# The last pair's feed-forward by batch, and the small steps of the norms moved between VectorE and GpSimd

## The chip, the cores and the metric

The kernel runs on one core of a Trainium2 chip. The metric is device time in microseconds (us) of one execution. The core's engines work in parallel, each through its own instructions in order: TensorE (PE; its weight loads are listed apart as PEld), VectorE (DVE), ScalarE (ACT), GpSimd (POOL), and SyncE (SP), which here only issues DMAs. Engines wait for one another through semaphores. Matrix products land in PSUM, which has eight banks of 128 partitions by 512 fp32 values; everything else lies in SBUF.

## The reference

The input is 16 batches of 256 tokens with 128 features. Twelve layers of linear attention (16 heads of 8, no softmax) are followed by a norm, a gated feed-forward network with hidden size 384, and a second norm:

```python
for i in range(12):
    q, k, v = split(x @ Wqkv[i].T + bqkv[i])        # 16 heads of 8
    att = einsum('bhqd,bhkd->bhqk', q, k) / sqrt(8)
    x = (att @ v) @ Wproj[i].T + bproj[i] + x
x = layernorm(x0 + x)                                # first norm
h = silu(x @ Wg.T / 127) * (x @ Wu.T / 127)
x = layernorm(x + h @ Wd.T / 127)                    # second norm
# layernorm(x) = (x - mean) / sqrt(var + 1e-5), over the 128 features
```

## The kernel before

The 16 batches are handled as eight pairs, numbered p = 0 to 7. A pair is 512 tokens: K = 4 chunks of 128 tokens. Since attention without softmax is linear, the twelve layers work on one small 128x128 map for each batch (a matrix `tst`, with one column for the offset); the tokens come in again only at the end, in `ffn(p)` (L567). The change concerns that function alone.

`ffn(p)` goes through these steps, all 512 tokens of a pair at once:

1. The map is transposed and copied, its offset column is split into three bf16 parts, and PE multiplies the tokens by it (L658). The result `pr` has tokens on the partitions and is already centred, because the last layer's weights had their mean taken off.
2. First norm, `norm(pr, True)` (L579): the statistics are two `bn_stats` on DVE, each over two chunks (L595). POOL then adds eps to the variance (`ve`, L602) and raises it to the power -0.5 (`rs`, L603). The scaling by `rs` is one DVE instruction (L608) or four ACT instructions (L613).
3. PE transposes the result back to features on the partitions (L664). To keep fp32 precision in fast products, every value that PE streams is split in two: a rounded high part (`xh`, a copy) and the rest (`xl`, a subtraction, L667).
4. For each of the three blocks of 128 hidden features: four products of 512 columns (gate and up, high and low part, L674 and L675), Silu on ACT (L677), the multiplication by up on DVE (L678), the split of the product into `hh` (a copy on ACT or DVE, L201 or L203) and `hl` (a subtraction on POOL or DVE, L206), and two products into the down sum (L686 and L687). The first block also adds `xl` times 127 (L685).
5. DVE scales the down sum and adds `xh` (L689). PE transposes back to tokens on the partitions (L695).
6. Second norm, `norm(po, False, po2)`: statistics, eps and power as in step 2. DVE then forms `nb`, the negated mean times the power (L621), and ACT scales each chunk with it, four instructions (L617), after which SP stores 256 KB (L701). For the last pair the transposed result lies in two banks: DVE scales chunks 0 and 1 (L615) and ACT chunks 2 and 3 (L617), and SP and ACT store 128 KB each.

Many of these values lie in buffers that earlier stages used, so the profile shows other names: `kv` is the normed value, `yhl` is `xh`, `thl` is `xl`, `xt` and `qgv` are the gated values.

The order of the work is not the order in which this code is written. Each step is registered with a planner (`Plan`, L92) with a booked duration for every engine that may do it, what it reads and writes, and a due time `prio`. `Plan.run` (L116) is a list scheduler: it takes the step that can start first, and among those that can start then the one with the smallest rank, puts it on the engine that it books to finish it first, and emits it there. The rank (L142) is the due time less a ten-thousandth of the booked nanoseconds that still follow the step on its longest path, with 300 ns for each step of the path:

```python
(_, end, e), o = min(((b, o) for b, o in found if b[0] <= first),
    key=lambda x: (x[1].prio - TAILW * x[1].tail, -x[1].tail, x[1].n))
```

A layer is one unit of due time; pair p of the feed-forward has 11 + 0.15 p. The eight PSUM banks are handed out by the planner too. All engines then run the emitted order as it is, so an instruction that waits holds back whatever was emitted behind it on its engine.

Of the kernel before, what the change touches and what calls it, by code (L numbers as in the profile page):

```python
# [9 lines left out]
F32 = mybir.dt.float32  # L10
# [42 lines left out]
TAILW = 0.0001  # L53

# [134 lines left out]
def linear_attention_ffn_kernel(ctx: ExitStack, tc: tile.TileContext, x, xt, wall, wq0, bias, wg, wu, wd, out):  # L189
# [360 lines left out]
    for p in range(NP):  # L550
# [4 lines left out]
            "ve": new(f"ve{p}", [4]), "rs": new(f"rs{p}", [4]), "nb": new(f"nb{p}", [4]), "st": new(f"st{p}", [K, 3]),  # L555
# [11 lines left out]
    def ffn(p, prio):  # L567
# [5 lines left out]
        v = {n: Val() for n in ("cr", "cp", "cq", "tt", "st", "rs", "nb", "x1", "xh", "xl", "sg0", "sg1", "hh0", "hh1", "hl0", "hl1")}  # L573
# [5 lines left out]
        def norm(src, centred, other=None):  # L579


            xs, rows = t("x1"), lambda: bank(src)
            cut = lambda a, k: a[:, k * C : (k + 1) * C]
            row = lambda k: cut(bank(other if other and k >= K // 2 else src), k)

            def stats(e):
                if e == ACT:
                    for k in range(K):
                        nc.scalar.activation(cut(xs, k), row(k), AF.Square, accum_out=t("st")[:, k, 2:3])
                else:  # L590

                    for k in range(0, K, 2):
                        b = bank(other if other and k else src)
                        both = b[:, k * C : (k + 2) * C].rearrange("p (k c) -> p c k", c=C)
                        nc.vector.bn_stats(t("st")[:, k : k + 2, :].rearrange("p k s -> p (k s)"), both)  # L595
            costs = {DVE: K // 2 * (dve(2 * C) + 70)}
            if centred:
                costs[ACT] = K * 485
            op(costs, stats, [src, *([other] if other else [])], [v["st"], v["x1"]])

            def rstd(e):
                nc.gpsimd.tensor_scalar(t("ve"), t("st")[:, :, 2], 1.0 / C, EPS, ALU.mult, ALU.add)  # L602
                nc.gpsimd.tensor_tensor(t("rs"), t("ve"), mhalf, ALU.pow)  # L603
            op({POOL: 1220}, rstd, [v["st"]], [v["rs"]])

            def scale(e, ks=range(K)):
                if centred and e == DVE:
                    nc.vector.tensor_tensor(chunks(xs), chunks(rows()), t("rs").unsqueeze(2).to_broadcast([128, K, C]), ALU.mult)  # L608
                    return
                for k in ks:  # L610
                    d, r, rs = cut(xs, k), row(k), t("rs")[:, k : k + 1]
                    if centred:
                        nc.scalar.activation(d, r, AF.Copy, scale=rs)  # L613
                    elif e == DVE:
                        nc.vector.tensor_scalar(d, r, t("st")[:, k, 1:2], rs, ALU.subtract, ALU.mult)  # L615
                    else:
                        nc.scalar.activation(d, r, AF.Identity, bias=t("nb")[:, k : k + 1], scale=rs)  # L617
            if centred:
                costs = {DVE: dve(N), ACT: K * act(C, False, 1)}
            else:  # L620
                op({DVE: 75}, lambda e: nc.vector.scalar_tensor_tensor(t("nb"), t("st")[:, :, 1], -1.0, t("rs"), ALU.mult, ALU.mult), [v["rs"], v["st"]], [v["nb"]])  # L621
                costs = {ACT: K * act(C, False, 2)}
            if not other:
                op(costs, scale, [src, v["rs"], v["st"], v["nb"]], [v["x1"]])
                return [v["x1"]]

            ends = [Val(), Val()]
            op({DVE: 2 * 319}, lambda e: scale(e, range(2)), [src, v["rs"], v["st"], v["nb"], v["x1"]], [ends[0]])
# [128 lines left out]
```

## Time and profile before

| | |
|---|---|
| median of 3 runs | 311.49 us (311.48 to 311.62) |
| profiled execution, its own time | 312.4 us |
| its span, first to last instruction | 310.7 us |
| mean granted TensorE clock | 0.988 |
| PE busy | 297.8 us, 96% |
| PEld busy | 272.5 us, 88% |
| DVE busy | 234.5 us, 75% |
| ACT busy | 212.5 us, 68% |
| POOL busy | 134.0 us, 43% |
| chain that ended last | PE 89%, DVE 5%, POOL 2%, issue 1%, DMA 1% |

The span is the time between the first and the last instruction; the execution's own time has what lies around it too. A row of the timeline gives start and length in us, engine, source line, operation, what it writes and reads (partitions x elements), how often, and in brackets how long the engine stood idle before it and what ended that. Instructions of one engine overlap in the records, since the next is started before the last has left the pipeline: how far two starts lie apart is then what an instruction costs its engine, and its length is what a reader of its result waits for. The chain of waits is followed back from the last instruction, at each step to what released it.

### The profile page before, as it was taken

To read this page: it belongs to the slowest core of one execution; us is meant where nothing else is said; L and a number is where in the kernel's file an instruction comes from. 1 tells how busy PE (TensorE), PEld (TensorE's weight loads), DVE (VectorE), ACT (ScalarE), POOL (GpSimd) and SP (SyncE) were. 2 spreads that over 40 slices of the span, in tenths; PEclk is the share of its full clock that TensorE was granted. 3 is DMA by queue.
4 is the path that set the end of the run, shared out by engine and by line. 5 is a ranking of instruction groups with operands and counts; after the bars stand their busy time and mean duration, and the time that the engine had idled before them with its cause. 6 is when DMAs were issued, how large, how long until landed. Compare 5 with 4: busy or idle time off the path is not lost.

```text
span 310.7 us, 12884 instructions
## 1 busy us (share of the span) xinstructions
PE 297.8 (96%) x5374; PEld 272.5 (88%) x5374; DVE 234.5 (75%) x706; ACT 212.5 (68%) x541; POOL 134.0 (43%) x218
## 2 busy tenths in 40 slices
PE   7997999999999999999999999999999999999971
PEld 7997999999999999989999999999999998887840
DVE  0788786977687676866768777676768798999982
ACT  2567797677677677666776767876876566657683
POOL 5337350545423454234531445312330459737781
PEclk9999999999999999999999999999999999999995
DMA  7464630211202012030120201300000000001124
GB/s 226 110 189 120 188 80 28 63 28 41 50 2 75 18 36 53 2 90 2 37 53 4 70 20 27 82 27 4 2 2 3 5 0 2 0 0 36 35 72 131
DMA packets 22490, 15.66 MB, mean 50 GB/s; under 512 B 1952, under 2 KB 19872, under 8 KB 22432
## 3 DMA queue, kind: packets, MB, share of 16 engines
q1 hardware_dynamic: 21872, 14.62, 17.1%
q8 instruction: 42, 0.69, 1.0%
q10 hardware_dynamic: 560, 0.22, 0.3%
q14 instruction: 16, 0.13, 0.2%
HBM read 8.02 MB, written 2.10 MB: 33 GB/s over the span
## 4 chain that ended last, share of the span: by engine, by line
PE 89%; DVE 5%; POOL 2%; issue 1%; DMA 1%; ACT 0%; POOLq 0%; DVEq 0%; ACTq 0%
PE bank L452 14%; PE bank L431 8%; PE bank L511 8%; PE bank L433 7%; PE bank L432 7%; PE bank L439 5%; PE bank L496 5%; PE bank L528 4%; PE bank L529 4%; PE bank L530 4%; PE bank L440 3%; PE bank L441 3%; PE bank L674 3%; PE bank L675 3%; PE bank L333 2%; PE bank L658 2%
## 5 line engine op out<-in xcount | busy, mean ns | idle before, releaser
L206 POOL TENSOR_TENSOR thl<-tst,thl 128x260 fp32r<-128x260 f32 x88 | 64.4, 763 | 122.9 <-ACT thl L201 122.9
L201 ACT COPY qgv<-bank 128x256 f32<-128x256 f32 x167 | 59.6, 376 | 20.8 <-PE bank L441 13.9
L201 ACT COPY kv<-bank 128x512 f32<-128x512 f32 (+1 forms) x89 | 51.0, 573 | 23.1 <-PE bank L433 16.4
L431 PE MATMUL bank<-whl,thl 128*128 128x256 f32 x176 | 51.8, 294 | 0.0
L433 PE MATMUL bank<-whl,thl 128*128 128x256 f32 x176 | 49.5, 281 | 0.0
L432 PE MATMUL bank<-whl,thl 128*128 128x256 f32 x176 | 49.4, 281 | 0.0
L452 PE MATMUL bank<-kv,g 128*128 128x128 f32 x352 | 46.4, 275 | 0.0
L535 DVE TENSOR_TENSOR tst<-bank,tst 128x260 f32<-128x260 f32 x96 | 36.7, 424 | 10.2 <-PE bank L530 8.6
L452 PEld LDWEIGHTS bank<-kv,g 128*128 128x128 f32 x352 | 42.9, 191 | 0.4 <-issue 0.4
L201 ACT CAST thl<-tst 128x260 fp32r<-128x260 f32 x88 | 33.1, 408 | 13.7 <-DVE tst L535 13.6
L445 DVE TENSOR_SCALAR qgv<-bank,bcol 128x2 f32<-128x2 f32 x88 | 19.3, 221 | 26.3 <-ACT qgv L201 21.4
L431 PEld LDWEIGHTS bank<-whl,thl 128*128 128x128 f32 x176 | 33.1, 188 | 4.1 <-issue 4.0
L524 DVE TENSOR_TENSOR yhl<-bank,yhl 128x260 fp32r<-128x260 f32 x96 | 34.1, 417 | 0.0
L432 PEld LDWEIGHTS bank<-whl,thl 128*128 128x128 f32 x176 | 33.2, 189 | 0.0
L433 PEld LDWEIGHTS bank<-whl,thl 128*128 128x128 f32 x176 | 33.1, 188 | 0.0
L439 PE MATMUL bank<-thl,whl 128*128 128x260 f32 x88 | 28.9, 329 | 0.0
L203 DVE CAST yhl<-bank 128x260 fp32r<-128x260 f32 (+1 forms) x49 | 19.4, 433 | 10.3 <-PE bank L511 10.2
L511 PE MATMUL bank<-qgv,gm 32*32 32x130 f32 x1536 | 26.2, 280 | 0.1
L201 ACT CAST yhl<-bank 128x260 fp32r<-128x260 f32 (+1 forms) x55 | 19.7, 402 | 7.5 <-PE bank L511 6.1
L440 PE MATMUL bank<-thl,whl 128*128 128x260 f32 x88 | 24.8, 282 | 0.0
L441 PE MATMUL bank<-thl,whl 128*128 128x260 f32 x88 | 24.7, 280 | 0.0
L511 PEld LDWEIGHTS bank<-qgv,gm 32*32 32x32 f32 x1536 | 17.3, 103 | 5.8 <-issue 0.7
(149 smaller groups left out, 702.3 us busy)
## 6 DMA issues: line engine op xcount, KB each, us to landing
wraw<-wall SPq DMA_DIRECT2D x12, 256.0 KB, 3.4
wpt<-whl SPq DMA_DIRECT2D x24, 96.0 KB, 2.3
qgv<-x SPq DMA_DIRECT2D x8, 256.0 KB, 5.1
xt<-xt SPq DMA_DIRECT2D x8, 256.0 KB, 4.4
out<-kv SPq DMA_DIRECT2D x7, 256.0 KB, 2.3
wpt<-whl SPq DMA_DIRECT2D x24, 64.0 KB, 2.1
wpt<-whl SPq DMA_DIRECT2D x24, 32.0 KB, 2.2
wraw<-wg SPq DMA_DIRECT2D x1, 192.0 KB, 4.2
```

The source lines that it names most:

```text
L201: nc.scalar.copy(dst, src)
L206: (nc.vector if e == DVE else nc.gpsimd).tensor_tensor(dst, a, b, ALU.subtract)
L431: nc.tensor.matmul(o, hi[:, b, 0:C], hl(0, 1, 2), start=True, stop=False)
L432: nc.tensor.matmul(o, hi[:, b, 0:C], hl(1, 1, 2), start=False, stop=False)
L433: nc.tensor.matmul(o, lo[:, b, 0:C], hl(0, 1, 2), start=False, stop=True)
L439: nc.tensor.matmul(o, hl(0, 0), flat(hi), start=True, stop=False)
L440: nc.tensor.matmul(o, hl(0, 0), flat(lo), start=False, stop=False)
L441: nc.tensor.matmul(o, hl(1, 0), flat(hi), start=False, stop=True)
L452: nc.tensor.matmul(bank(pgv)[:, b * C : (b + 1) * C], g0[p][:, b, :], tv(b), start=True, stop=True)
L511: nc.tensor.matmul(bank(pys[r])[group(g + r), b * W : (b + 1) * W], gm[group(g), r * PB + b, :], qss[p][group(g), b, :], start=True, stop= ...
L524: plan.op({DVE: dve(PB * W)}, lambda e: nc.vector.tensor_tensor(yl, bank(py)[:, : PB * W], yh.bitcast(F32), ALU.subtract), [py, vyh[p]], [ ...
L535: plan.op({DVE: dve(PB * W)}, lambda e: nc.vector.tensor_tensor(ts, bank(pw)[:, : PB * W], ts, ALU.add), [pw], [vt[p], vc[p]], prio)
```

## The change

Two things are changed.

First, the small steps of both norms. eps is added by DVE, behind the `bn_stats` and in the same step, and no longer by POOL. For the second norm DVE also forms the negated mean `nm` there, and POOL multiplies it by the power to get `nb`, in the same step as the power; DVE's instruction for `nb` is gone. This holds for all eight pairs. The statistics of the first norm can no longer be put on ACT. The booked durations of these steps are changed with it.

Second, what follows the first norm is a function of its own, `unit`. Pairs 0 to 6 call it once, for all four chunks. The last pair calls it twice, for chunks 0 and 1 (one batch) and for chunks 2 and 3 (the other), with everything at half width: 256 columns in the products and in the instructions between them, 128x2 in the small steps. Both units have a due time that is 0.2 earlier (`AHEAD`). The first batch ends as other pairs do: ACT scales both chunks and SP stores 128 KB. For the second batch, PE transposes chunk 3 once more into a bank of its own (`again`); DVE scales chunk 2 from the first bank, ACT scales chunk 3 from the other, and SP and ACT store 64 KB each.

```diff
+AHEAD = 0.2
...
-        def norm(src, centred, other=None):
+        def norm(v, src, ks, centred, again=None, op=op):
...
             def stats(e):
-                if e == ACT:
-                    for k in range(K):
-                        nc.scalar.activation(cut(xs, k), row(k), AF.Square, accum_out=t("st")[:, k, 2:3])
-                else:
-
-                    for k in range(0, K, 2):
-                        b = bank(other if other and k else src)
-                        both = b[:, k * C : (k + 2) * C].rearrange("p (k c) -> p c k", c=C)
-                        nc.vector.bn_stats(t("st")[:, k : k + 2, :].rearrange("p k s -> p (k s)"), both)
-            costs = {DVE: K // 2 * (dve(2 * C) + 70)}
-            if centred:
-                costs[ACT] = K * 485
-            op(costs, stats, [src, *([other] if other else [])], [v["st"], v["x1"]])
+
+                for k in ks[::2]:
+                    both = cut(bank(src), k - ks[0], 2).rearrange("p (k c) -> p c k", c=C)
+                    nc.vector.bn_stats(t("st")[:, k : k + 2, :].rearrange("p k s -> p (k s)"), both)
+                nc.vector.tensor_scalar(of("ve"), of("st")[:, :, 2], 1.0 / C, EPS, ALU.mult, ALU.add)
+                if not centred:
+                    nc.vector.tensor_scalar(of("nm"), of("st")[:, :, 1], -1.0, None, ALU.mult)
+            op({DVE: n // 2 * (dve(2 * C) + 40) + 75 * (2 - centred)}, stats, [src], [v["st"]])
 
             def rstd(e):
-                nc.gpsimd.tensor_scalar(t("ve"), t("st")[:, :, 2], 1.0 / C, EPS, ALU.mult, ALU.add)
-                nc.gpsimd.tensor_tensor(t("rs"), t("ve"), mhalf, ALU.pow)
-            op({POOL: 1220}, rstd, [v["st"]], [v["rs"]])
+                nc.gpsimd.tensor_tensor(of("rs"), of("ve"), mhalf[:, :n], ALU.pow)
+                if not centred:
+                    nc.gpsimd.tensor_tensor(of("nb"), of("nm"), of("rs"), ALU.mult)
+            op({POOL: 380 + 170 * n + 220 * (not centred)}, rstd, [v["st"]], [v["rs"]])
...
-                op({DVE: 75}, lambda e: nc.vector.scalar_tensor_tensor(t("nb"), t("st")[:, :, 1], -1.0, t("rs"), ALU.mult, ALU.mult), [v["rs"], v["st"]], [v["nb"]])
-                costs = {ACT: K * act(C, False, 2)}
-            if not other:
-                op(costs, scale, [src, v["rs"], v["st"], v["nb"]], [v["x1"]])
-                return [v["x1"]]
-
+                costs = {ACT: n * act(C, False, 2)}
+            if not again:
+                op(costs, scale, [src, v["rs"], v["st"]], [v["x1"]])
+                return [(ks, v["x1"])]
             ends = [Val(), Val()]
-            op({DVE: 2 * 319}, lambda e: scale(e, range(2)), [src, v["rs"], v["st"], v["nb"], v["x1"]], [ends[0]])
-            op({ACT: 2 * act(C, False, 2)}, lambda e: scale(e, range(2, K)), [other, v["rs"], v["st"], v["nb"], v["x1"]], [ends[1]])
-            return ends
+            op({DVE: 319}, lambda e: scale(e, ks[:1]), [src, v["rs"], v["st"], v["x1"]], [ends[0]])
+            op({ACT: act(C, False, 2)}, lambda e: scale(e, ks[1:], lambda k: bank(again)[:, :C]), [again, v["rs"], v["x1"]], [ends[1]])
+            return [(ks[:1], ends[0]), (ks[1:], ends[1])]
...
-        norm(pr, True)
+        norm(v, pr, range(K), True)
+        if p < NP - 1:
+            unit(p, v, range(K), op, norm, True)
+        else:
+
+            ahead = lambda costs, emit, reads, writes: plan.op(costs, emit, reads, writes, prio - AHEAD)
+            for b in range(PB):
+                unit(p, dict(v, **{n: Val() for n in UNIT}), range(2 * b, 2 * b + 2), ahead, norm, b < PB - 1)
...
+    def unit(p, v, ks, op, norm, inner):
+
+        m, k0 = len(ks) * C, ks[0]
+        t = lambda n: ctxs[p][n][:, k0 * C : k0 * C + m]
+        x1 = ctxs[p]["x1"]
+        px, pd, po = (Val("bank") for _ in range(3))
+        again = None if inner else Val("bank")
+        of = lambda a: bank(a)[:, :m]
...
+                    nc.tensor.matmul(of(o), ws, t("xh"), start=True, stop=False)
+                    nc.tensor.matmul(of(o), ws, t("xl"), start=False, stop=True)
+                op({PE: 2 * mmr(m)}, mm_x, [v["xh"], v["xl"], vfw[key]], [o])
...
+        def tr_o(e, ks=ks, to=po, k0=k0):
+            for k in ks:
+                nc.tensor.transpose(bank(to)[:, (k - k0) * C : (k - k0 + 1) * C], ctxs[p]["sg0"][:, k * 128 : (k + 1) * 128], ident)
+        op({PE: len(ks) * 109}, tr_o, [v["sg0"]], [po])
+        if again:
+            op({PE: 109}, lambda e: tr_o(e, ks[1:], again, ks[1]), [v["sg0"]], [again])
+        for i, (kk, end) in enumerate(norm(v, po, ks, False, again, op)):
+            def store(e, r0=p * N + kk[0] * C, n=len(kk) * C, src=x1[:, kk[0] * C : (kk[-1] + 1) * C]):
+                (nc.sync if e == SP else nc.scalar).dma_start(out[r0 : r0 + n, :].rearrange("(k p) c -> p k c", p=128), src.rearrange("p (k c) -> p k c", c=C))
+            op({(ACT if i else SP): 2.6 * len(kk) * C}, store, [end], [])
```

## The prediction

> **What bounds the kernel now.** I read the page first, then the stretches of the last 70 us, then the chain of waits, and last the instructions in order of time. The page's slices show PE full to the 39th of 40, so most of the span is PE work that the change leaves as it is.
>
> ```profile
> PE   7997999999999999999999999999999999999971
> DVE  0788786977687676866768777676768798999982
> ```
>
> The stretches by time (the first number after each window is its length, then busy us of PE, PEld, DVE, ACT, POOL, the granted clock and DMA):
>
> ```profile
> core 0: us, PE busy (x) PEld busy (x) DVE busy (x) ACT busy (x) POOL busy (x), PEclk, DMA share, GB/s
> 270.00:280.00 10.00, 10.00 (x49) 8.18 (x48) 9.67 (x17) 6.11 (x12) 4.17 (x5) 1.00 0.00 0
> ...
> 285.00:290.00 5.00, 5.00 (x25) 4.11 (x25) 4.97 (x10) 3.01 (x6) 4.05 (x4) 1.00 0.18 52
> 290.00:295.00 5.00, 5.00 (x27) 4.04 (x26) 4.97 (x12) 4.29 (x9) 3.35 (x5) 1.00 0.19 54
> 295.00:300.00 5.00, 4.45 (x26) 3.41 (x23) 5.00 (x13) 4.05 (x11) 4.34 (x6) 1.00 0.20 54
> 300.00:305.00 5.00, 2.40 (x8) 1.28 (x7) 3.11 (x10) 4.45 (x13) 2.56 (x4) 0.81 0.55 150
> 305.00:311.00 6.00, 0.00 (x0) 0.00 (x0) 0.97 (x4) 0.81 (x2) 1.21 (x2) 0.50 0.34 93
> ```
>
> Two engines are full together until about 299 us: PE, and VectorE (DVE). ScalarE (ACT) and GpSimd (POOL) have room. After 299 us no engine is full: the last 12 us are the drain of the last pair. The chain of waits names its links (start, length, what):
>
> ```profile
> 300.38 1.01 POOL rs L603
> 301.39 0.26 POOL ve L602
> 301.72 1.02 POOL rs L603
> ...
> 302.76 0.16 DVE nb L621
> 302.93 0.61 DVE xt L689
> ...
> 303.58 0.70 PE bank L695 x2
> ...
> 304.31 0.87 DVE st L595 x2
> ...
> 305.25 0.20 POOL ve L602
> ...
> 305.49 1.06 POOLq L753
> ...
> 306.58 0.17 DVE nb L621
> ...
> 306.83 0.81 ACT kv L617 x2
> ```
>
> L689 starts behind an nb that belongs to another pair. In order of time the last down product and what DVE did next read:
>
> ```profile
> 301.63 0.50 PE L687 MATMUL bank<-hl,wfd 128*128 128x512 f32 x1 [0.84 <-DVE hl L206]
> 301.72 1.01 POOL L603 TENSOR_TENSOR rs<-ve,mhalf 128x4 f32<-128x4 f32 x1
> 302.76 0.16 DVE L621 SCALAR_TENSOR_TENSOR nb<-st,rs 128x4 f32<-128x4 f32 x1 [1.11 <-POOL rs L603]
> 302.84 0.68 DVE L689 SCALAR_TENSOR_TENSOR xt<-bank,yhl 128x512 f32<-128x512 f32 x1
> ```
>
> L687 ends at 302.13, yet L689 starts at 302.84: DVE stands 1.11 us at an nb that waits for POOL's power, and L689 is queued behind it.
>
> **The end, link by link.** *L689 at half width*: 0.68 us now; the nearest row of half the width is L524, 128x260, 0.42 us: -0.26. *nb leaves DVE*: L689 no longer stands behind POOL. It may start 0.07 after L687, at 302.2: -0.6. Next late is L687 itself. *Statistics to power*: now 304.31 to 305.54, 1.23 us (two bn_stats, eps on POOL, two hops). After: one bn_stats 0.42, eps on DVE with a read-after-write gap 0.04 and 0.15 long, the negated mean 0.07 behind it, hop 0.08, sum 0.76: -0.47. *The power* takes 1.01 for 128x4 in all but a few of 16; for 128x2 no row exists. Ends: 0.20 (POOL's 128x4 tensor_scalar, L602) and 1.01 (nothing saved). I take 0.70, just above the middle, as nearer to the row of the same operation: -0.3; ends -0.8 and 0. *nb on POOL*: now 306.58 to ACT's start at 306.83, 0.25; after, POOL 0.20 plus gap 0.07 and hop 0.08, 0.35: +0.10. DVE's scale needs only the power and not nb. *Scale*: one instruction for each engine in place of two, ACT 0.84 to 0.46 and a 0.03 hop: -0.35. *Stores*: 128 KB takes 2.0 us to land and 256 KB 2.3; 64 KB is booked at -0.1, ends -0.3 and 0. SP issues two of the last pair's three stores where it issued one (0.37 us each); the first is out before the end, and the second waits behind whatever store precedes it on SP. *The repeated transpose* of the last 128 tokens lies on PE while DVE takes the statistics; ACT reads it over 1 us later: 0; were that cover gone, 0.1 us. Sum: -0.26 - 0.6 - 0.47 - 0.3 + 0.1 - 0.35 - 0.1 = -2.0.
>
> **The last pair in halves, before that.** PE: 19 products of 512 columns come 0.234 us apart; those of 260 come 0.117 to 0.12 apart (L439 to L441 near 151.5 us), so 38 halves cost about 0.1 more, the repeated transpose 0.1: +0.2, on PE, which is the bound. DVE: instructions of 512 columns come 0.60 apart, of 260 0.333 apart (L524 at 248.33, four in 1.42), so a split adds 0.07; about eight of the pair's are on DVE (L667, three L678, L689, some hh and hl): +0.56. ACT's splits have room: it is busy 61 to 86% there; without room each is 0.07 or so. POOL's hl goes from 1.27 to about 0.75 for a half, two for one: +0.2, also in room. *The drain*: the last L678, hh, hl and L687 become half as long, together about -0.9 (0.26 + 0.17 + 0.25 + 0.2) if they follow one another directly; today 297.86 to 301.63 holds 2.6 us of other pairs' DVE work between them. Ends -0.9 and 0; I take -0.45.
>
> The row just used meets a rule that speaks against the split. The Trainium skill's "VectorE: DVE Perf Modes", section on the TRN2 errata, advises tiles of at least 512 elements, because a fixed cost is paid per instruction, and gives about 150 cycles for it; at the page's 0.96 GHz that is, as an estimate, 0.156 us an instruction, 1.25 us for eight splits. The trace's 0.07 between starts (0.16 only if durations are added instead, 2 x 0.42 against 0.68) makes it 0.56; by the page's figure the sum below would end 0.7 higher at most, if nothing hid it.
>
> **Small instructions on DVE, all pairs.** A 128x4 one costs 0.07 between independent starts (L337 to L338 at 10.62 and 10.69). One that reads the instruction just ahead waits longer: hh behind L678 starts 0.72 after it (272.60 to 273.32) against 0.60, so 0.12. That the first norm's statistics lose ACT as a choice costs nothing: all 32 bn_stats are on DVE now. Eight first norms gain eps: 8 x 0.19 = +1.5. Nine second norms (seven pairs and two halves) gain eps and the negated mean, and eight nb go: 9 x 0.26 - 8 x 0.08 = +1.7. With the splits DVE gains 3.8 us. The bookings that the planner uses for the DVE statistics hardly rise (812 to 827 ns for a first norm; 812 + 75 to 902 with the nb for a second), so it will not push hh or hl to ACT or POOL on this account. Who hides it: up to 299 us PE is full and on the chain, and DVE's other short idle stretch, 0.58 us at 282.5, also an nb waiting for POOL, goes. What lies after PE's end is in the open: the norm groups at 296.60, 299.13 and 300.24, 3 x 0.18, and three splits, 0.21: +0.75. Ends: 0, and 1.7 if everything from 270 on lands (1.7 + 0.56 - 0.58). I take +0.75, the part that lies behind PE. Behind a late DVE instruction stand the stats, L678 and L667, for which PE and ACT wait.
>
> POOL loses 16 eps instructions (0.2 to 0.3) and gets nine nb products of that size; no difference on its part of the chain. Its power waits for DVE as its eps did; behind it stand hl subtractions, as now.
>
> *Order.* The planner ranks by due time less a ten-thousandth of the booked ns still ahead. For the last pair's transposes after the first norm that booked rest falls from about 17.0 to 12.0 us by adding the code's costs with 300 ns a step: rank 0.50 later, and AHEAD takes back 0.20. At the last L689 it is 11.39 against 11.40, unchanged, so the last half should stay behind pair 6. The order in between changes freely; I book 0, with 1 us either way, about the spread of three neighbouring second norms (gaps 2.5, 1.1, 4.1 us).
>
> Sum against the profiled execution (span 310.7, its time 312.4, so 1.7 lies outside): -2.0 + 0.2 + 0.75 - 0.45 = -1.5, so 309.2 of span and 310.9. That execution is 0.9 above the median of the runs, 311.49; from the median the forecast is **310.0**.
>
> **The rivals.**
> *A: as summed*, 310.0; own range 309.2 to 310.9.
> *B: the two halves hide each other.* DVE's extra lands nowhere, the drain gives its whole 0.9: -2.0 + 0.2 - 0.9 = -2.7. But pair 6 is not split: its scale on ACT ends at 304.65, its store is issued at about 305.1 and lands 2.3 later, and the program ends 1.0 after the last landing (307.67 + 2.0 = 309.7 against 310.7): 308.4. So at most -2.3: 309.2. For: ACT and POOL have room. Against: DVE is at 97% or more.
> *C: no difference.* All of DVE's late 1.7 lands and the drain gives nothing: -2.0 + 0.2 + 1.7 = -0.1, 311.4.
> *D: slower, DVE becomes the bound of the whole feed-forward stage.* From 240 to 303 us it is busy 57.67 of 63.00 us. If all 3.8 land, the two nb stalls apart: -2.0 + 0.2 + 3.8 - 0.6 = +1.4, 312.9. It decides from 2.4 us landed on, and shows as slower from 3.0. For: the planner does not see the extra. Against: 5.3 us are free there, and PE is the chain until 277.
> *E: the change does not shorten the end,* because pair 6, unsplit, becomes last in the old last place: from 302.2, L689 with its hop 0.74, transposes 0.73, statistics to power 1.1, power 1.04, nb 0.35, four scales 1.5, store 3.3: 8.8, so 311.0 of span, +0.3, 311.8. Against: the ranks above.
>
> **How the numbers follow.** A 0.44, B 0.24, C and E together 0.12, D 0.20. A kernel of this spread can be told from no change by about 0.2%, 0.6 us. A and B are faster: 0.68. C and E lie within: 0.12. D: 0.20. The range runs from 308.4, below B by the power's lower end (a further 0.5) and the rest of the order's, to 312.4, which leaves out the upper two thirds of D (0.13) and some 0.05 below.
>
> **What would show it.** Right: no nb on DVE; L689 of the last half starts within 0.2 us of its L687; a 128x2 power of about 0.7; from the last L689's start to the end 6.5 us in place of 7.9; PE full until 299 us again. Wrong: DVE without a gap while PE shows idle time behind L206, L678 or L667 before 295 us (D); the last scale group being four instructions (E); last-pair transposes (L664) much later than 281 us with PE waiting (the order); a power that keeps its 1.01.

## The result, and the profile after

| | before | changed |
|---|---|---|
| median, runs on the same chip | 311.49 us (311.11 to 311.62) | 312.94 us (312.81 to 313.22) |
| profiled execution, its own time | 312.4 us | 312.81 us |
| its span | 310.7 us | 311.1 us |
| DVE busy | 234.5 us | 238.8 us |
| POOL busy | 134.0 us | 129.6 us |

The changed kernel is **slower by 1.45 us: ratio 1.005, 95% interval 1.0033 to 1.0067.** On another chip it gave 313.45 against 311.71, 1.0063 (1.0047 to 1.0078). The forecast was 310.0, faster, with 312.4 as its upper end.

The two profiled executions are not equally typical of their kernels: that of before lies 0.9 above its median. The following two views show where, and give the measure used from here on. They are the groups of the first product with the low part in the centring of the last layer's weights, first of the kernel before, then of the changed one (times are first to last start):

```profile
L533 PE MATMUL bank<-thl,centerr x8: 277/283/285, 236.7 to 252.0; 128*128 128x260 f32 x8
```

```profile
L534 PE MATMUL bank<-thl,centerr x8: 277/280/285, 235.7 to 249.5; 128*128 128x260 f32 x8
```

As many of PE's instructions come ahead of this product in both kernels, and all but the last three of them are the same, yet the execution of before reached it 1.0 us later. From here to the end of the span is **the stage** in what follows: 310.7 - 236.7 = 74.0 us before, 311.1 - 235.7 = 75.4 us after. Its +1.4 agrees with the +1.45 of the medians, while the spans alone (+0.4) would hide most of it.

Engines by stretches of time, changed kernel (columns as in the prediction):

```profile
core 0: us, PE busy (x) PEld busy (x) DVE busy (x) ACT busy (x) POOL busy (x), PEclk, DMA share, GB/s
270.00:280.00 10.00, 10.00 (x48) 8.00 (x49) 9.86 (x19) 6.19 (x12) 3.85 (x3) 1.00 0.00 0
280.00:285.00 5.00, 3.94 (x20) 2.92 (x19) 4.84 (x12) 3.38 (x8) 2.22 (x4) 1.00 0.02 3
285.00:290.00 5.00, 5.00 (x25) 4.10 (x24) 4.93 (x11) 4.13 (x10) 4.62 (x5) 1.00 0.17 46
290.00:295.00 5.00, 5.00 (x28) 4.14 (x27) 4.68 (x12) 2.95 (x8) 4.04 (x5) 1.00 0.29 82
295.00:300.00 5.00, 4.83 (x30) 3.65 (x28) 4.81 (x14) 4.12 (x11) 3.21 (x4) 1.00 0.21 59
300.00:305.00 5.00, 2.46 (x14) 1.61 (x14) 4.70 (x18) 4.07 (x12) 3.14 (x5) 1.00 0.38 105
305.00:311.00 6.00, 0.43 (x3) 0.19 (x3) 1.08 (x4) 1.85 (x5) 1.55 (x4) 0.60 0.40 109
```

The row of before that the prediction leaves out:

```profile
280.00:285.00 5.00, 4.73 (x25) 3.71 (x24) 4.42 (x11) 3.56 (x9) 3.96 (x4) 1.00 0.02 3
```

In the changed kernel PE is busy for only 3.94 of the 5.00 us from 280, where it had 4.73 before. DVE shows 4.84 in that row, so it looks like the bound there. The chain of waits shows what that busy time is:

```profile
281.07 0.35 DVE st L593
...
281.45 1.29 DVE ve L594
282.74 0.07 DVE nm L596
282.81 0.60 DVE xt L693
...
283.45 0.50 PE bank L689
```

`ve` is the eps step, two numbers in each partition. It is on the chain with 1.29 us; the last product before it started at 282.00, and PE waits until 283.45. In the group of this line it is an outlier (count, then shortest, median and longest in ns):

```profile
L594 DVE TENSOR_SCALAR ve<-st x17: 169/170/1292, 242.7 to 305.8; 128x4 f32<-128x4 f32 x15, 128x2 f32<-128x2 f32 x2
```

In order of time, the changed kernel's DVE and POOL at this place and at another:

```profile
266.42 1.28 POOL L207 TENSOR_TENSOR hl<-xt,hh 128x512 fp32r<-128x512 f32 x1 [0.57 <-DVE hh L204]
266.60 1.39 DVE L207 TENSOR_TENSOR hl<-xt,hh 128x256 fp32r<-128x256 f32 x1
...
281.43 1.28 POOL L207 TENSOR_TENSOR hl<-xt,hh 128x512 fp32r<-128x512 f32 x1 [3.56 <-ACT hh L202]
281.45 1.29 DVE L594 TENSOR_SCALAR ve<-st 128x2 f32<-128x2 f32 x1
```

POOL's subtraction ends at 267.70 and 282.71. DVE's two, which take 0.42 and 0.17 elsewhere, end 0.29 and 0.03 after it: **they end only when POOL's subtraction beside them has ended.** What a DVE instruction lasts beyond its form elsewhere is called its stretch below (elsewhere: `ve` 0.17, `nb` 0.16, `hh` 0.28 at 256 columns and 0.43 at 512, `hl` 0.42 and 0.69). In the stage it adds up to 3.1 us in the changed kernel. The same pattern was in the trace of before, in order of time there:

```profile
270.31 1.30 POOL L206 TENSOR_TENSOR hl<-xt,hh 128x512 fp32r<-128x512 f32 x1 [0.19 <-ACT hh L201]
270.69 1.20 DVE L203 CAST hh<-xt 128x512 fp32r<-128x512 f32 x1
...
285.87 1.28 POOL L206 TENSOR_TENSOR hl<-xt,hh 128x512 fp32r<-128x512 f32 x1 [0.92 <-ACT hh L201]
...
286.57 1.13 DVE L206 TENSOR_TENSOR hl<-xt,hh 128x512 fp32r<-128x512 f32 x1
```

There it adds up to 1.4 us. The change raised it by 1.7.

The end of the changed kernel in order of time:

```profile
303.42 0.75 DVE L593 BATCH_NORM_STATS2 st<-bank 128x6 f32<-128x256 f32 x2
...
303.56 0.38 PE L702 MATMUL bank<-hl,wfd 128*128 128x256 f32 x1
304.20 0.17 DVE L594 TENSOR_SCALAR ve<-st 128x4 f32<-128x4 f32 x1
304.28 0.16 DVE L596 TENSOR_SCALAR nm<-st 128x4 f32<-128x4 f32 x1
304.36 0.42 DVE L704 SCALAR_TENSOR_TENSOR xt<-bank,yhl 128x256 f32<-128x256 f32 x1
...
305.77 1.85 ACT L616 ACTIVATE kv<-bank,nb,rs 128x128 f32<-128x128 f32 x5 [1.01 <-POOL nb L602]
...
306.08 0.70 POOL L600 TENSOR_TENSOR rs<-ve,mhalf 128x2 f32<-128x2 f32 x1 [0.34 <-DVE nm L596]
...
306.81 0.41 DVE L614 TENSOR_SCALAR kv<-bank,st,rs 128x128 f32<-128x128 f32 x1 [0.74 <-POOL rs L600]
...
307.30 0.92 SPq L714 DMA_DIRECT2D out<-kv  x2
307.65 0.38 ACTq L714 DMA_DIRECT2D out<-kv  x1
```

From the start of the last scaling of a down sum (L689 before, L704 after) to the end of the span it takes 311.1 - 304.36 = 6.74 us, where it took 310.7 - 302.84 = 7.86. So the shorter end is there, worth 1.1 us. But its start has moved: 302.84 - 236.7 = 66.1 us into the stage before, 304.36 - 235.7 = 68.7 after. The loss of 2.5 us lies ahead of the last pair's end.

### The profile page after: what moved, and what is told of

The parts are those of the page before. It is cut to its first block, busy times and chain, and to the rows that moved or that the text cites. A ratio compares the mean times of both kernels' runs of the same rounds, so it can differ in the third digit from the quotient of the medians.

```text
span 311.1 us, 12949 instructions
## 1 busy us (share of the span) xinstructions
PE 298.7 (96%) x5394; PEld 273.3 (88%) x5394; DVE 238.8 (77%) x734; ACT 212.9 (68%) x548; POOL 129.6 (42%) x210
## 4 chain that ended last, share of the span: by engine, by line
PE 86%; DVE 10%; DMA 1%; ACT 1%; issue 1%; POOL 0%; DVEq 0%
PE bank L453 14%; PE bank L432 8%; PE bank L512 8%; PE bank L434 7%; PE bank L433 7%; PE bank L440 5%; PE bank L497 5%; PE bank L529 4%; PE bank L530 4%; PE bank L531 4%; PE bank L442 3%; PE bank L441 3%; PE bank L334 2%; PE bank L378 2%; PE bank L689 2%; PE bank L690 2%
## 5 line engine op out<-in xcount | busy, mean ns | idle before, releaser
L202 ACT CAST yhl<-bank 128x260 fp32r<-128x260 f32 (+2 forms) x57 | 20.8, 405 | 8.5 <-PE bank L512 6.3
L204 DVE CAST yhl<-bank 128x260 fp32r<-128x260 f32 x48 | 18.3, 423 | 10.0 <-PE bank L512 10.0
L600 POOL TENSOR_TENSOR rs<-ve,mhalf 128x4 f32<-128x4 f32 (+1 forms) x17 | 17.8, 1047 | 13.2 <-DVE ve L594 8.0
```

What stands on the lines that cost most here:

```text
L202: nc.scalar.copy(dst, src)
```

## The experiments

Three theories of that loss, under the letters that the expectations use:

- **P**, held by POOL: a DVE instruction that reads and writes SBUF, begun while a long POOL subtraction runs, ends only after it (below: the holding); the change lets more of them meet.
- **D**, DVE's work: the added small instructions and splits themselves make DVE late.
- **O**, the order: the last pair's first batch runs too early, ahead of all pairs. In the trace its second norm comes at 281 us, before that of any other pair. The code has a reason: the value `x1` is not in `UNIT`, so both units share it. The last scaling of the first unit writes it and the transposes of the second read it, so in the planner's books all of the second batch follows the whole first batch.

Stage and stretch are read from the one profiled execution of each run, the ratio from all its timed runs. Repeats of the stage agreed within 0.1 us in three cases and within 0.7 in one (small steps alone). That one shows what else moves the stage. The last product of the down sum and the last four transposes, in order of time, first in the shorter execution and then in the longer one:

```profile
303.33 0.50 PE L691 MATMUL bank<-hl,wfd 128*128 128x512 f32 x1 [1.04 <-DVE hl L206]
304.62 0.66 PE L699 MATMUL bank<-ident,xt 128*128 128x128 f32 x4 [0.78 <-DVE xt L693]
```

```profile
303.25 0.80 PE L691 MATMUL bank<-hl,wfd 128*128 128x512 f32 x1 [1.04 <-DVE hl L206]
304.83 1.12 PE L699 MATMUL bank<-ident,xt 128*128 128x128 f32 x4 [0.78 <-DVE xt L693]
```

The granted clock from 304 to 306 us was 1.00 in the first and 0.50 in the second. With the slow transposes the eps step behind them starts 1.62 us after the first of them, in place of 1.27; the slow product costs 0.30 more: together the whole difference. A star marks the stages whose last transposes were slow (1.12 for the four; in before too). At the full clock these would be, as an estimate from such rows, 73.6 for before, 75.0 for the repeat of the small steps, and 72.9 twice for the small steps without subtractions (the second has 0.14 on the product too). In the repeat of the changed kernel the last three transposes take 0.87 in place of 0.52, but its stage is as long.

| kernel | ratio to before, 95% | stage, us | stretch, us |
|---|---|---|---|
| before | 1 | 74.0* | 1.4 |
| changed, and again | 1.005 (1.0033, 1.0067); 1.0063 (1.0047, 1.0078) | 75.4; 75.4* | 3.1; 3.1 |
| before, no POOL subtractions, and again | .9991 (.9975, 1.0007); .9996 (.9976, 1.0016) | 72.4; 72.3 | 0; 0 |
| changed, no POOL subtractions | .9974 (.9949, .9999) | 72.2 | 0 |
| small steps alone, and again | 1.005 (1.0035, 1.0065); 1.0051 (1.0031, 1.007) | 75.0; 75.7* | 2.6; 2.6 |
| small steps alone, no POOL subtractions, and again | 1.0005 (.9983, 1.0026); 1.0008 (.9993, 1.0023) | 73.3*; 73.4* | 0; 0 |
| split alone | 1.001 (.9991, 1.0029) | 74.2 | 3.9 |
| split alone, no POOL subtractions | .9976 (.9965, .9986) | 71.9 | 0 |
| changed, batches freed | .9977 (.9953, 1.0002) | 72.3 | 0.8 |
| changed, batches freed, no POOL subtractions | .9975 (.9964, .9986) | 71.8 | 0 |
| freed, planner told of the holding, AHEAD 0.25 | **.9943 (.9922, .9963)** | 72.3 | 0.6 |
| the same, AHEAD 0.3 | .9953 (.9933, .9973) | 72.4 | 1.2 |

### Without POOL's subtractions

The feed-forward's `hl` on POOL becomes a power of about the same length over 6 columns (2 for a half); on DVE it stays a subtraction. The planner's books, and so the order, stay as they are. The `hl` tiles are set to zero by POOL in the earlier layers, which is more work ahead of the stage, so the ratio of these kernels to before is not the effect of the edit alone. They are compared with one another and by the stage.

```diff
+    def low(e, dst, a, b):
+        n = 6 if a.shape[1] == 512 else 2
+        if e == DVE:
+            nc.vector.tensor_tensor(dst, a, b, ALU.subtract)
+        else:
+            nc.gpsimd.tensor_tensor(dst[:, :n], b[:, :n], mpow[:, :n], ALU.pow)
...
-            op({POOL: pool(m), DVE: dve(m)}, lambda e, ...: sub(e, t(hlo), t(sg), t(hh).bitcast(F32)), ...)
+            op({POOL: pool(m), DVE: dve(m)}, lambda e, ...: low(e, t(hlo), t(sg), t(hh).bitcast(F32)), ...)
```

Before, expected:

> The kernel before, in its own order, with each feed-forward subtraction that POOL does (1.28 us at 512 columns, the low part hl) replaced by a POOL power of the same length on 6 columns of hh (the low part is left out of the result, apart from zeros). Theory P (DVE's SBUF-to-SBUF instructions stand still while POOL runs a long subtraction): the trace of before has two such stretched DVE instructions (hl 1.13 in place of 0.69 at 286.57, hh 1.20 for two casts at 270.69 in place of 0.85), about 0.8 us in all, so this kernel is 0 to 0.8 us faster than before. Theory D (the number of DVE instructions decides) and theory O (the order of the last pair's halves decides): no change, within 0.4 us.

Changed, expected:

> The changed kernel, in its own order, with the same replacement of POOL's feed-forward subtractions by powers of the same length (the low part is left out). Theory P: the trace of the changed kernel has four stretched DVE instructions behind POOL's subtractions (ve 1.29 in place of 0.17 at 281.45, hl 1.39 in place of 0.42 at 266.60, hh 0.74 in place of 0.28 at 271.30, hh 0.60 in place of 0.42 at 263.88), 2.7 us together, so this kernel falls by 1.5 to 2.7 us against the changed one, to 310.3 to 311.4, at or below before. Theories D and O: it stays at 312.5 to 313.

Measured: 311.36 us, which fits all three theories, and 310.93 us, which fits P alone. The stage falls from 74.0 to 72.4 before, and from 75.4 to 72.2 after. The edit takes 1.6 us off the one (1.3 at the full clock) and 3.2 off the other, about what each had of stretch (1.4 and 3.1). With the subtractions the change costs 1.4 us (1.8 at the full clock); without them it gains 0.2 (and 0.9974 against 0.9991 on one chip, with overlapping intervals). The changed kernel without them, in order of time, at the two places shown above:

```profile
266.79 1.32 POOL L214 TENSOR_TENSOR hl<-hh,mpow 128x6 fp32r<-128x6 f32 x1 [0.54 <-DVE hh L204]
266.97 0.43 DVE L212 TENSOR_TENSOR hl<-xt,hh 128x256 fp32r<-128x256 f32 x1
...
280.38 1.32 POOL L214 TENSOR_TENSOR hl<-hh,mpow 128x6 fp32r<-128x6 f32 x1 [3.10 <-ACT hh L202]
280.42 0.18 DVE L608 TENSOR_SCALAR ve<-st 128x2 f32<-128x2 f32 x1
```

POOL is as long busy at the same two places, and DVE's instructions beside it take 0.43 and 0.18 instead of 1.39 and 1.29. So it is not POOL's being busy that holds DVE, but POOL's subtraction over 512 columns. P holds, and **the holding turns a gain of about 0.2 us into a loss of 1.4 to 1.8.** But without it the gain is 0.2 and not the 1.5 of the forecast; that is the second question.

The rule that the trace shows here stands in the Trainium skill, "SBUF — State Buffer", section "SBUF: two separate sides": a pair of ports is shared by VectorE and GpSimd as an exclusive lock, held for a whole instruction, and the loser stands still. The subtraction agrees (1.39 and 1.29 beside 1.28). The power of 1.32 us does not: beside it DVE took 0.43 and 0.18, and here the measurement decides.

### The small steps alone

Kernel before with eps and the negated mean on DVE and the product on POOL; no split; order and books held, with an empty step where DVE formed `nb`.

```diff
                         nc.vector.bn_stats(...)
+                    nc.vector.tensor_scalar(t("ve"), t("st")[:, :, 2], 1.0 / C, EPS, ALU.mult, ALU.add)
+                    if not centred:
+                        nc.vector.tensor_scalar(t("nm"), t("st")[:, :, 1], -1.0, None, ALU.mult)
...
-                nc.gpsimd.tensor_scalar(t("ve"), t("st")[:, :, 2], 1.0 / C, EPS, ALU.mult, ALU.add)
                 nc.gpsimd.tensor_tensor(t("rs"), t("ve"), mhalf, ALU.pow)
+                if not centred:
+                    nc.gpsimd.tensor_tensor(t("nb"), t("nm"), t("rs"), ALU.mult)
...
-                op({DVE: 75}, lambda e: nc.vector.scalar_tensor_tensor(t("nb"), ...), ...)
+                op({DVE: 75}, lambda e: None, ...)
```

> The small steps alone: eps and the negated mean by DVE behind the statistics, the product with the power by POOL, no split of the last pair; the bookings are those of before and an empty step keeps nb's place, so the order of everything else is that of before. Theory D: DVE's extra (0.19 for each of 8 first norms, 0.26 less 0.08 for each of 8 second norms, 3 us) lands for the larger part: 312.5 to 313.5. Theory P: only collisions count; in the order of before one eps lands under a subtraction (near 286.6), where another DVE instruction was held already: 310.9 to 311.9, with the 0.6 us wait of L689 behind nb gone. Theory O: as P, since the last pair is whole.

Measured 313.17, and stage 75.0: slower by the whole amount of the change. That is D's number and not P's, though P had counted too few meetings: 2.6 us of stretch came out. One of them, in order of time of this kernel:

```profile
285.99 1.29 POOL L206 TENSOR_TENSOR hl<-xt,hh 128x512 fp32r<-128x512 f32 x1 [1.38 <-ACT hh L201]
286.15 1.16 DVE L596 TENSOR_SCALAR ve<-st 128x4 f32<-128x4 f32 x1
```

The same without POOL's subtractions, to see D alone:

> The small steps alone in the order of before (as in the run of that name), with POOL's feed-forward subtractions replaced by powers of the same length (the low part is left out). Its twin is the kernel before with the same replacement, in the same order, whose time from the first centring product of the last layer to the end was 72.4 us. Theory P: the stretch of 2.6 us that the small steps alone showed goes, so that time is 72.1 to 72.7, equal to its twin's within 0.3. Theory D: the 3 us of DVE instructions that the twin has not cost 1.0 to 1.4 as they did with the subtractions: 73.4 to 73.8.

Measured: stage 73.3, against 72.4 of its twin without the small steps (72.9 at the full clock that its twin had). That is above P's range, which ends at 72.7, and below D's, which begins at 73.4. Both were repeated on one chip:

> The kernel before without POOL's long subtractions (the low part is left out), again, on one chip with its twin that follows. 0.997 to 1.001 of before, as in the first run of it.

> The small steps alone in the order of before, without POOL's long subtractions (the low part is left out), beside its twin. If DVE's 3 us of further instructions land in part even without collisions (theory D in part, as the first run hinted), 0.4 to 1.0 us slower than the twin; if the first run's difference was that of two chips, within 0.3 us of it (theory P alone).

> The small steps alone in the order of before, with the subtractions, for the comparison on the same chip: 1.3 to 1.7 us slower than before, with eps held at the same two places (near 260.7 and 286.2 us, 0.6 and 1.0 us).

Measured on one chip: 311.97 with the small steps against 311.25 without, **+0.7 us**, as expected of D in part; by the stage 73.4 against 72.3, +1.1, of which the slower clock makes up 0.5. With the subtractions the small steps gave 313.58 against 311.66, +1.9, more than the 1.3 to 1.7 expected (the first time +1.4; stage 75.0 both times at the full clock, with the same stretch at the same places). So the moved steps cost 0.5 to 0.7 us by DVE's work, end included; the holding adds the rest, 0.7 to 1.2 by the medians and 0.8 to 0.9 by the stage at the full clock, where the stretch rose by 1.2.

Where the 0.5 to 0.7 lie is seen in the two later traces without subtractions, which begin the stage at 237.4 and 237.5. With the small steps the last product of the down sum ends at 303.09; in the twin at 301.73. Counted from the start of the stage that is 1.4 us later; 0.14 of it is the slower clock (the product takes 0.64 in place of 0.50), and **1.3 us** is left. Then the twin stands 0.71 us (its `nb` waits for a power, as in before) and scales at 302.44; with the small steps the scaling starts 0.03 after the product. So the wait that the change removes is gone, and gives back half of what DVE's work had cost until there.

### The split alone

Changed kernel with the small steps as before: eps on POOL ahead of the power, `nb` on DVE.

```diff
                     nc.vector.bn_stats(...)
-                nc.vector.tensor_scalar(of("ve"), of("st")[:, :, 2], 1.0 / C, EPS, ALU.mult, ALU.add)
-                if not centred:
-                    nc.vector.tensor_scalar(of("nm"), of("st")[:, :, 1], -1.0, None, ALU.mult)
...
+                nc.gpsimd.tensor_scalar(of("ve"), of("st")[:, :, 2], 1.0 / C, EPS, ALU.mult, ALU.add)
                 nc.gpsimd.tensor_tensor(of("rs"), of("ve"), mhalf[:, :n], ALU.pow)
...
+                op({DVE: 75}, lambda e: nc.vector.scalar_tensor_tensor(of("nb"), of("st")[:, :, 1], -1.0, of("rs"), ALU.mult, ALU.mult), ...)
```

> The split alone: the changed kernel with the small steps as before (eps on POOL, nb on DVE), with the old bookings for them; DVE has some 3 us less to do than in the changed kernel. Theory D: 0.5 to 1.5 us faster than before. Theory P: it goes by the collisions of its own order, of which the planner's books show more than in any other order (8.0 us of DVE instructions with both operands in SBUF planned under a POOL subtraction, against 4.7 in the changed kernel and 0.9 with the batches freed): a stretch of 2 to 4 us in the trace and a time from the first centring product to the end of 72.3 plus that stretch, 74.3 to 76.3; slower than before by 0.5 to 2 us.

Measured 312.11, ratio 1.001 (0.9991 to 1.0029): no difference that can be told, so not the gain that D expected; P's slowdown isn't shown by the ratio either. Its stage, 74.2, lies just below P's range. Its stretch is the largest of all, 3.9 us; one copy of 0.43 us takes 1.45. Without POOL's subtractions:

> The split alone with the small steps as before, and POOL's feed-forward subtractions replaced by powers of the same length (the low part is left out). With the subtractions its trace showed 4.0 us of stretch and 74.2 us from the first centring product to the end. Theory P: most of the stretch comes back, 70.5 to 72 us, 0.990 to 0.996 of before. Theory D has no reason for any change: 73.8 to 74.6.

Measured: stage 71.9, within P's range and not D's, though the ratio, 0.9976, gained less than P said. It is 0.4 less than in the kernel before without subtractions (72.3), and 2.3 less than with them, not the whole stretch of 3.9. The split gains, but 0.4 us and not much more, even without the holding.

### The batches freed of each other

The second unit gets an `x1` of its own in the planner's books, written by the first norm alone. The instructions are the same; only their order changes.

```diff
-                unit(p, dict(v, **{n: Val() for n in UNIT}), range(2 * b, 2 * b + 2), ahead, norm, b < PB - 1)
+                own = Val()
+                own.writers = list(v["x1"].writers)
+                unit(p, dict(v, x1=own, **{n: Val() for n in UNIT}), range(2 * b, 2 * b + 2), ahead, norm, b < PB - 1)
```

> The changed kernel with one edit: the planner no longer makes the second batch's transposes wait for the first batch's last scale (the two share the value x1 in the planner's books, though they write different halves), so the halves may run side by side and the first is no longer pulled to the front of all pairs. Theory O: 310.0 to 311.2, faster than before, with the first batch's second norm near the end and not at 281 us. Theory D: 312.5 to 313.5, as the DVE instructions are the same. Theory P: open, since the order changes and with it the collisions; it follows the sum of the stretched DVE instructions, about 1 us of time for each 1.5 us of them beyond those of before.

Measured 310.56, ratio 0.9977; stage 72.3, 3.1 less than the changed kernel. That would fit O, if the stretch had stayed. It fell to 0.8: the new order lets few meet. So the two were parted by taking POOL's subtractions away here too, with the changed kernel beside it again:

> The changed kernel with the batches freed, and POOL's feed-forward subtractions replaced by powers of the same length (the low part is left out). Its twin without the freeing took 72.2 us from the first centring product to the end, 0.9974 of before. Theory O (that the first batch goes ahead of all pairs and the second waits for it costs time by itself): 0.6 to 1.5 us less than the twin, 0.992 to 0.996. Theory P: the freed kernel gained by its few collisions alone, so this one equals its twin, within 0.4 us.

> The changed kernel itself, beside the two that follow, for the comparison on one chip: 1.003 to 1.007 of before, with the same stretched DVE instructions at the same places as in its first trace, 2.5 to 3.5 us, since the order is fixed (theory P).

Measured: stage 71.8, against 72.2 of the changed kernel without them, within what P allowed and short of what O expected; the ratios, 0.9975 and 0.9974 on different chips, show no difference. **The order by itself is worth 0.4 us at most;** the other 2.7 of the freeing came through the stretch. The changed kernel itself gave 75.4 again, with the same five stretched instructions at the same places, so the holding belongs to the order and isn't chance.

### The planner told of the holding

If P is the cause, a planner that knows of it should find an order without. Freed as above; the planner keeps the end of POOL's last booked `hl`, starts DVE's `hh` and `hl` no earlier, and lets DVE's statistics step end no earlier than 170 ns after it.

```diff
+                    if e == DVE and o.port == "all":
+                        t = max(t, held_by_pool)
+                    elif e == DVE and o.port == "end":
+                        c = max(c, held_by_pool + 170 - t)
...
+            if e == POOL and o.port == "all":
+                held_by_pool = end
```

> The changed kernel with the batches freed of one another in the planner's books, and with the planner told of the shared port: a DVE copy to hh or subtraction to hl is not planned to start while a planned POOL subtraction runs, and statistics are booked to end after it; AHEAD is 0.25. The books then show no overlap. Theory P: a stretch under 0.6 us, a time from the first centring product to the end of 71.5 to 72.5, and 1.5 to 2.3 us faster than before. Theory D: no gain over the kernel with the batches freed alone, within 0.5 us of before.

> As the run before it, with AHEAD 0.3: another order, with 0.6 us of planned overlap. Theory P: a stretch of 0.3 to 1.0 us, 71.6 to 73.0 from the first centring product to the end, 1 to 2.2 us faster than before. Theory D: within 0.5 us of before.

Measured 310.04 us (309.20 to 310.28) with AHEAD 0.25, against 311.53: **ratio 0.9943 (0.9922 to 0.9963), better than both kernels**; 310.08 and 0.9953 with AHEAD 0.3, where the stretch was 1.2, more than expected. The eps steps of the former, as a group:

```profile
L602 DVE TENSOR_SCALAR ve<-st x17: 170/170/171, 241.9 to 302.6; 128x4 f32<-128x4 f32 x15, 128x2 f32<-128x2 f32 x2
```

None of the 17 is stretched. Its stretches of time:

```profile
280.00:285.00 5.00, 5.00 (x25) 4.10 (x24) 4.86 (x12) 4.96 (x13) 2.87 (x5) 1.00 0.19 52
290.00:295.00 5.00, 5.00 (x35) 4.48 (x34) 4.97 (x14) 4.55 (x13) 3.71 (x6) 1.00 0.24 67
295.00:300.00 5.00, 4.43 (x32) 3.72 (x30) 4.93 (x19) 4.05 (x12) 3.82 (x6) 1.00 0.19 54
300.00:305.00 5.00, 1.26 (x7) 0.83 (x7) 3.10 (x13) 3.95 (x11) 3.58 (x8) 0.72 0.37 105
```

DVE shows 4.86 from 280 to 285, as much as in the changed kernel (4.84), but here it works, and PE is full. From 300 to 305 PE has 1.26 us left to do where it had 2.46. How much of the gain over the freed kernel (310.04 against 310.56, on different chips and with overlapping intervals) is due to the books isn't shown; the stage is 72.3 in both, and the gap of 0.5 us is about what D allowed for.

## Why the prediction was wrong

**The sum.** Forecast -1.5, measured +1.45. Of the 2.95 between them, the runs put 1.6 to the holding (+1.4 with it, -0.2 without; at the full clock +1.8 and so 2.0). The other 1.3 lie between the -1.5 of the forecast and the -0.2 without the holding: the steps below. These were measured in different orders and don't add up to the 1.3 term by term.

**The step that failed: "Small instructions on DVE, all pairs".** It took 0.07 to 0.12 us for each small instruction from rows of other places, and summed only what lies on DVE. What it left out is that an eps step on DVE waits for POOL's subtraction when the two meet: +1.12 and +0.36 for two of the 17 in the changed kernel. It could have been read in the trace of before: a copy of 1.20 and a subtraction of 1.13, both beside a POOL subtraction and both on an engine that the prediction called full. They were read as DVE's busy time. POOL was looked at only for its own load ("no difference on its part of the chain"), not for what it does to DVE.

Without the holding the term was still mis-sized. Of its +0.75 "in the open", 0.54 was for the small steps (3 x 0.18), the part behind PE's end; the upper end was 1.7. Measured, in the order of before: the last product ends 1.3 us later by them. PE's being full up to 299 us, but for the short gaps in its rows, did not hide them.

**"Order", booked at 0 with 1 us either way.** The ranks were worked out as if the second batch depended on the first norm alone. The shared `x1` made it wait for the whole first batch in the books, so the work booked behind the first batch's transposes is 23.6 us, where the prediction had 12.0 for the last pair's; the first batch ran ahead of all pairs, and pair 6 and the second batch met at the end. By itself that costs 0.4 us at most. Through the meetings that this order makes, it costs up to 2.7 more: the same instructions in the freed order have 0.8 of stretch instead of 3.1. The planner books a gain from the change (306.73 to 306.07 us in its own reckoning), because it knows no holding.

**"The end, link by link", -2.0.** The mechanism was right: no `nb` is left on DVE, the 128x2 power takes 0.70 as taken, eps and the negated mean lie 0.08 apart. From the start of the last L704 to the end of the last scale (307.62) it takes 3.26 us, where it took 4.80 before: -1.54, of which the slow transposes of before are 0.35; the terms gave -1.28. What was mis-sized is the stores, booked at -0.1: from the end of the last scale to the end of the span it takes 3.48 us, and 3.06 before. ACT's 64 KB take 2.2 us to land, and its 128 KB took 2.0 before. And SP's second store, as the prediction named but priced at nothing, "waits behind whatever store precedes it on SP". Chunk 2 is ready at 306.81 + 0.41 = 307.22; pair 6's 256 KB are issued on SP at 307.30, and the two SP issues end together at 308.22. The second takes 0.46, so it begins at 307.76. That the whole, 6.74 us, came so near the 6.5 of the terms is in part luck: the clock gave 0.35, and the stores took 0.5 more than booked.

The term for L689's start, -0.6, came out at half of that, -0.29: the last L704 starts 0.42 after its product ends (303.56 + 0.38 = 303.94), in place of 0.71, because pair 6's statistics, eps and negated mean stand ahead of it. Next late was not L702, as the prediction had it, but the group of the pair that it had called safely ahead.

**"The drain", -0.45.** Not seen: the last L704 starts 2.5 us later in the stage. Even without the holding the split alone gains 0.4 us in all, end and drain together.

**The rivals.** D gave 312.9, 0.04 from what was measured, with DVE as the bound. The number is a coincidence. Its mechanism, 3.8 us of DVE's own work landing in full, doesn't hold: without POOL's subtractions the changed kernel, which has nearly all of that work, gains 0.2. Its sign on the trace ("DVE without a gap while PE shows idle time behind L206, L678 or L667 before 295 us") was there at 282 to 283 us, because an instruction that is held counts as busy. B and C fell with the sum. (B's bound of 308.4 counts pair 6's store from 305.1; in before it is issued at 304.68, which with 2.3 and 1.0 gives 308.0.) E was half right: pair 6 does end with the last batch, and its store makes the last one wait for 0.46 us. The 2.5 us lost ahead of the end are no part of E.

## What to carry to other kernels

Before work is put on VectorE, look in the profile for VectorE instructions with SBUF on both sides that last longer than others of their shape, and at what GpSimd does beside them; such an engine is "busy" with waiting, and one more small instruction can last as long as GpSimd's longest subtraction. Read the longest of a group beside its median: 170 and 1292 ns told the story here. When a list scheduler gives an odd order, look for a value that two independent units share, and put into its books what the engines do to each other, or it can book gains that the chip doesn't have.

## What the runs showed of the hardware that was not expected

- An instruction of 128x2 elements on DVE takes 1.29 us in place of 0.17 when it begins 0.02 us after a POOL subtraction of 1.28 us; the length of the wait is set by POOL's instruction and not by DVE's.
- The holding goes both ways: in the changed kernel a POOL subtraction that starts at 286.87, 0.10 after a DVE copy of 0.43, takes 1.48 in place of 1.28 to 1.30.
- DVE instructions that read PSUM aren't held: in the changed kernel the subtraction L682, from 275.75, takes its 0.68 while POOL subtracts from 275.32 to 276.62.
- A POOL power of the same length holds nothing (0.43 and 0.18 beside 1.32). The other way round it seems to suffer itself, as these rows of the changed kernel in order of time show:

```profile
289.61 0.68 DVE L207 TENSOR_TENSOR hl<-xt,hh 128x512 fp32r<-128x512 f32 x1
289.71 1.69 POOL L600 TENSOR_TENSOR rs<-ve,mhalf 128x4 f32<-128x4 f32 x1
```

The 128x4 power takes 1.01 elsewhere; begun beside a DVE subtraction it takes 1.69. In every trace here the 128x4 powers begun beside a DVE `hl` of 512 columns last 1.33 to 1.75; no run took that apart.
